# Scores and mix in smaller steps, the mask on the way out of PSUM, and norms by Ln, Exp and one Newton step, in a planned transformer kernel

## The chip, the cores and the metric

The kernel runs on one core of a Trainium2 chip. The time is the device time of one execution in microseconds (us); the time before is the median of three runs.

Five engines matter here. PE (TensorE) multiplies matrices and transposes; its products land in PSUM. DVE (VectorE), ACT (ScalarE) and POOL (GpSimd) work element by element, and SP issues transfers. Each engine runs its own list of instructions in order. An instruction whose input is not ready, or whose output buffer is still in use, holds up everything behind it in the same list.

## What is computed

Sixteen sequences of 256 tokens, 128 wide, go through two layers. The first part (a linear attention, a mixture of experts, and a causal linear attention with learned features) is not touched by the change. The last part is a stack of six blocks of windowed attention and a gated feed-forward layer, and the change is in its attention:

```python
def attn_layer(x, Wqkv, qs, ksc, Wo):
    q, k, v = ...                       # 16 heads of 64
    q = l2norm(q) * qs                  # l2norm(t) = t / max(norm(t), 1e-12)
    k = l2norm(k) * ksc
    q = q * cos * scale + rotate_half(q) * sin * scale
    k = k * cos / scale + rotate_half(k) * sin / scale
    out = local_attention(q, k, v)      # windows of 32, each sees itself and the one before
    return out @ Wo

# in local_attention
sim = einsum("bhwie,bhwje->bhwij", bq, bk2) * 8.0
sim = where(mask, -max_float, sim)
attn = softmax(sim, -1)
out = einsum("bhwij,bhwje->bhwie", attn, bv2)

for i in range(6):
    x = attn_layer(shift_tokens(x), ...) + x
    x = ffn_layer(shift_tokens(x), ...) + x
```

All arithmetic is in float32.

## The kernel before

Four stages follow each other. The first three (linear attention, experts, causal attention) take up to about 1650 us. The fourth is the stack of six blocks; there are 8 units of two sequences, and a sequence has two tiles of 128 tokens. So each block has 32 tiles in 8 units, and the whole stage has 192 tiles in 48 units.

The fourth stage is not written in the order in which it runs. Every piece of work is declared as a `Step` with its engine, a booked duration, the steps that it waits for, the buffers that it takes and a rank. `Plan.run` then plays a clock through these booked durations and lets each free engine take the ready step of lowest rank whose buffers are free. What comes out is a fixed list per engine, emitted in a manual schedule (L1155). A finished step makes its successors ready after `LAG` (L68), 0.12 us for every engine; a switch of ACT's function table is booked at `SWITCH`, 1.3 us. The plan's clock decides the lists only; on the chip the engines wait for each other by semaphores, by the real durations. Buffers come in kinds with few slots (L694 to L709): four PSUM pairs of 1024 columns, two `e`, four `t1`, two `sq` and so on. A step that takes a PSUM pair can start only when the steps that use its earlier content are through. Work on a later tile is let in three tiles ahead (`AHEAD`, and `gate` at L1114).

One tile goes through these steps, the names being those of the code:

- `projections` (L738): PE multiplies the 128 tokens by the weights of q, and then of k, into a PSUM pair each (L748). ACT squares the pair (L801), DVE multiplies it by the cosine table (`first`, L755) and, with halves swapped, by the sine table (`second`, L762), and reduces the squares per head (L771). POOL adds the two products (L810).
- `norms` (L773) calls `inv_norm` (L724) on DVE for q and k together, 128 by 32 values: a floor (L726), a first guess from the bits of the number (L729), and three Newton steps of three instructions (L733 to L735). POOL scales q and k by it (L777), PE transposes both (L783), ACT copies them to `qT` and `kT` (L789).
- `attention` (L836): `scores` (L843) is one PE step with 64 small products; 32 tokens see 64 keys, for 16 heads and 4 windows. DVE adds the mask in PSUM (`mask`, L860), takes the maximum per row (`top`, L864), and subtracts it on the way to `e` in SBUF (`below`, L869). ACT takes the exponential (L878).
- PE multiplies the value products (L885), ACT copies them to `va` (L892); PE transposes `e` (L899), ACT copies that to `eT` (L956). `mix` (L904) is 32 small products for each half of the heads (L911), two PE steps per tile. DVE divides by the sums (`divide`, L922 and L923), PE transposes, ACT copies to `oT` (L929).
- Per sequence `output` (L979) multiplies by Wo (L985) and DVE adds to the residual (L994). Per unit `feed_forward` (L1000) follows, with a norm, three gates with the gelu function on ACT, and products on PE (L1011, L1044, L1064).

In the records a float32 product shows as two MATMUL rows and two weight loads (LDWEIGHTS, engine PEld). ACT's table loads are put in when the program is built, ahead of a function that is not in the table loaded last.

Of the kernel before, what the change touches and what calls it, by code (L numbers as in the profile page):

```python
# [17 lines left out]
P = 128  # L18
# [31 lines left out]
class Step:  # L50


    def __init__(self, eng, work, fn, after, takes, uses, rank, table):
        self.eng, self.work, self.fn, self.rank = eng, work, fn, rank
        self.takes, self.uses, self.table = takes, uses, table
        self.next, self.wait = [], 0
        for b in (*takes, *uses):
            b.left += 1
        for s in after:
            s.next.append(self)  # L60
            self.wait += 1


class Plan:

    LAG = 0.12  # L68
    SWITCH = 1.3

    def __init__(self, slots):
        self.slots, self.steps, self.tick = slots, [], 0
        self.free = {k: list(range(len(v))) for k, v in slots.items()}

    def step(self, eng, work, fn, after=(), takes=(), uses=(), rank=0, table=None):
        s = Step(eng, work, fn, [a for a in after if a is not None], takes, uses, rank, table)
        self.steps.append(s)
        return s
# [30 lines left out]
    def run(self):  # L109
# [5 lines left out]
        for n, s in enumerate(self.steps):  # L115
# [3 lines left out]
            if not s.wait:  # L119
                heapq.heappush(ready[s.eng], (s.rank, n, s))  # L120
        now, table, opened = 0.0, None, {}
        left = len(self.steps)
        self.log = []
        while left:
            moved = True
            while moved:
                moved = False
                for eng, heap in ready.items():
# [40 lines left out]
                    at[eng] = now + work  # L169
                    heapq.heappush(events, (now + work + self.LAG, count, got))  # L170
                    heapq.heappush(events, (now + work, count + 1, None))
# [3 lines left out]
            while events and events[0][0] <= now:  # L175
# [31 lines left out]
def tile_kernel(ctx: ExitStack, tc: tile.TileContext, a: dict, out: bass.AP):  # L207
# [469 lines left out]
    with ExitStack() as st:  # L677
# [45 lines left out]

        def inv_norm(x, n):  # L724

            dve.tensor_scalar(x, x, 1e-24, None, ALU.max)  # L726
            y = sd.tile([P, n], F32, name="d_ny")
            t = sd.tile([P, n], F32, name="d_nt")
            dve.tensor_scalar(  # L729
                y.bitcast(I32), x.bitcast(I32), -0.5, 1597463007.0, ALU.mult, ALU.add  # L730
            )
            for _ in range(3):
                dve.tensor_tensor(t, y, y, ALU.mult)  # L733
                dve.scalar_tensor_tensor(t, t, -0.5, x, ALU.mult, ALU.mult)
                dve.scalar_tensor_tensor(y, t, 1.5, y, ALU.add, ALU.mult)  # L735
            return y

        def projections(q, t):  # L738
# [33 lines left out]

            def norms():  # L773
                o.rn = inv_norm(o.ss.rearrange("p g h -> p (g h)"), 2 * HEADS)

# [17 lines left out]
            for qk in range(2):  # L793
                pj, sq, t1, t2 = Buf("pair"), Buf("sq"), Buf("t1"), Buf("t2")
                mm = step(
                    "pe", 1.72, partial(product, qk, pj), [*q.ready, *q.loaded, q.gate(t)],
                    [pj], rank=rank,
                )
# [21 lines left out]
            for qk in range(2):  # L820
                dst, off = (q.kT, WIN + t * P) if qk else (qT, 0)
                pz = Buf("pair")
                m = step("pool", 1.9, partial(scale, qk, t1s[qk]), [nm, adds[qk]], [], [t1s[qk]], rank)
                tn = step("pe", 0.88, partial(turn, t1s[qk], pz), [m], [pz], [t1s[qk]], rank)
# [11 lines left out]
        def attention(q, t):  # L836
# [5 lines left out]

            def scores():  # L843

                for c in range(8):
                    for par in range(2):
# [11 lines left out]
            def mask():  # L858
                s3 = pS.t.rearrange("p (h k) -> p h k", k=2 * WIN)
                dve.tensor_tensor(s3, s3, bc(win[:, t, :], [P, HEADS, 2 * WIN], 1), ALU.add)  # L860

            def top():
                o.m = sd.tile([P, HEADS], F32, name="d_m")
                dve.tensor_reduce(  # L864
                    o.m, pS.t.rearrange("p (h k) -> p h k", k=2 * WIN), AX.X, ALU.max
                )

            def below():
                dve.tensor_tensor(  # L869
                    e.t.rearrange("p c a k -> p a c k"),  # L870
                    pS.t.rearrange("p (a c k) -> p a c k", a=2, k=2 * WIN),
                    bc(o.m.rearrange("p (a c) -> p a c", a=2), [P, 2, 8, 2 * WIN], 3),
                    ALU.subtract,
                )

# [27 lines left out]

            def mix(hh, po):  # L904
                for k in range(4):
                    c = 4 * hh + k
# [26 lines left out]

            sc = step("pe", 1.9, scores, [o.done[0], *q.turned[: t + 1]], [pS], [qT, kT], rank)
            mk = step("dve", 1.15, mask, [sc], [], [pS], rank)
            tp = step("dve", 1.15, top, [mk], [], [pS], rank)
            be = step("dve", 1.15, below, [tp], [e], [pS], rank)
            ex = step("act", 0.98, exps, [be], [], [e], rank, ("exp", 0))
            q.soft.append(be)
            vs = []  # L940
            for b2 in range(NB // 2):
                pv = Buf("pair")
                v = step(
                    "pe", 1.94, partial(values, b2, pv), [*q.ready, *q.loaded, mk], [pv], [], rank
                )
# [6 lines left out]
            pz = Buf("pair")  # L952
            te = step("pe", 0.88, partial(turn, e, pz), [ex], [pz], [e], rank)
            pe_ = step(
# [4 lines left out]
            for hh in range(2):  # L959
                po = Buf("pair")  # L960
                mx = step("pe", 0.75, partial(mix, hh, po), [pe_, *vs], [po], [eT, va], rank)
                ds.append(
                    step(
                        "dve", 0.85, partial(divide, hh, po), [mx],
                        [] if hh else [y], [po] + ([y] if hh else []), rank,
                    )
                )
            py = Buf("pair")
            ty = step("pe", 0.88, partial(turn, y, py), ds, [py], [y], rank)
            if t == 0:  # L970
# [8 lines left out]
        def output(q):  # L979
# [16 lines left out]
            rank = q.rank + 1  # L996
            mm = step("pe", 3.5, product, [*q.outs, *q.loaded], [pr], [q.oT], rank)
            return step("dve", 0.9, add, [mm], [], [pr], rank)
# [267 lines left out]
```

## Time and profile before

| | us |
|---|---|
| median of three runs (lowest, highest) | 5855.04 (5848.07, 5859.02) |
| the profiled execution, its own time | 5849.97 |
| its span in the profile | 5848.2 |
| PE busy | 4866.8 (83%) |
| DVE busy | 4182.3 (72%) |
| ACT busy | 2325.8 (40%) |
| POOL busy | 1951.1 (33%) |

Busy times are sums over the whole span. A matmul's end is modelled, so that a busy PE is not PE at its peak. The groups of instructions (line, engine, operation, output and input, count; busy us and mean ns of one; idle time before them and what ended it) give the durations of the fourth stage:

```profile
L810 POOL TENSOR_TENSOR d_t<-d_t,d_t 128x1024 f32<-128x1024 f32 x384 | 905.3, 2363 | 1717.1 <-DVE d_t L762 1242.4
L777 POOL TENSOR_TENSOR d_t<-d_t,d_ny 128x1024 f32<-128x1024 f32 x384 | 722.7, 1903 | 520.4 <-DVE d_ny L735 515.9
L771 DVE TENSOR_REDUCE d_ss<-d_sq 128x16 f32<-128x1024 f32 x384 | 464.9, 1211 | 1.4
L851 PE MATMUL pp<-d_kT,d_qT 64*32 64x64 f32 x24576 | 309.2, 232 | 157.2 <-issue 103.8
L911 PE MATMUL pp<-d_va,d_eT 64*32 64x65 f32 x24576 | 301.1, 228 | 85.5 <-issue 41.5
```

"issue" is time in which the engine waited for nothing that the profile shows.

### The profile page before, as it was taken

The page shows a single profiled execution, that of the slowest core. Times are in us where ns is not written, and L with a number is a line of the kernel's source. Part 1 is how long each engine was busy: PE and PEld are TensorE (multiplying, and loading weights), DVE is VectorE, ACT ScalarE, POOL GpSimd, SP SyncE. Part 2 cuts the span into 40 slices and gives each one's busy share as a digit, 9 for nine tenths or more (in the row PEclk, how much of TensorE's full clock was granted, in tenths as well). Part 3 has the DMA queues.
Part 4 walks back from the last instruction along what each step waited for, and adds up shares of the span by engine and source line. Part 5 has one row for each costly group of instructions (what it writes and reads, how often), then busy time and mean ns, then how long its engine had stood idle before and what let it go on. Part 6 is the DMA issues. An engine that isn't in the chain of part 4 may idle for free. (4 is left out here: it accounts for less than half of the span.)

```text
span 5848.2 us, 153345 instructions
## 1 busy us (share of the span) xinstructions
PE 4866.8 (83%) x69216; PEld 3086.3 (53%) x69216; DVE 4182.3 (72%) x7764; ACT 2325.8 (40%) x2701; POOL 1951.1 (33%) x964
## 2 busy tenths in 40 slices
PE   4677778787788888888888888898898888888886
PEld 3444566566655555555555555555555555555554
DVE  3333777777777777777678777777777777777775
ACT  1343112111134444444444444444444444444443
POOL 0000222222234344344344334334334434434432
PEclk7898899999999999999999999999999999999998
DMA  1000000000000000000000000000000000000001
GB/s 37 13 1 20 1 2 2 4 3 2 2 25 2 2 2 13 10 2 2 2 17 6 2 2 2 21 2 2 2 2 21 2 2 2 2 2 2 2 2 30
DMA packets 29195, 40.16 MB, mean 7 GB/s; under 512 B 5118, under 2 KB 24060, under 8 KB 27772
## 3 DMA queue, kind: packets, MB, share of 16 engines
q1 hardware_dynamic: 28540, 30.35, 1.7%
q8 instruction: 543, 8.90, 0.6%
q14 instruction: 112, 0.92, 0.1%
HBM read 26.15 MB, written 4.19 MB: 5 GB/s over the span
## 5 line engine op out<-in xcount | busy, mean ns | idle before, releaser
L810 POOL TENSOR_TENSOR d_t<-d_t,d_t 128x1024 f32<-128x1024 f32 x384 | 905.3, 2363 | 1717.1 <-DVE d_t L762 1242.4
L777 POOL TENSOR_TENSOR d_t<-d_t,d_ny 128x1024 f32<-128x1024 f32 x384 | 722.7, 1903 | 520.4 <-DVE d_ny L735 515.9
L748 PE MATMUL pp<-d_wqkv,xs 128*128 128x512 f32 x1536 | 776.4, 636 | 85.0 <-ACT d_oT L929 49.6
L885 PE MATMUL pp<-d_wqkv,xs 128*64 128x512 f32 x3072 | 753.5, 624 | 76.2 <-DVE d_t L762 75.2
L755 DVE TENSOR_TENSOR d_t<-pp,d_tab 128x1024 f32<-128x1024 f32 x384 | 467.8, 1218 | 392.7 <-PE pp L748 392.6
L801 ACT ACTIVATE d_sq<-pp 128x1024 f32<-128x1024 f32 x384 | 388.6, 1025 | 756.2 <-PE pp L748 250.6
L892 ACT COPY d_va<-pp 128x1024 f32<-128x1024 f32 x384 | 383.5, 1011 | 530.5 <-PE pp L885 529.5
L783 PE MATMUL pp<-ident,d_t 128*128 128x128 f32 x3072 | 414.0, 282 | 119.5 <-ACT d_qT L789 85.3
L762 DVE TENSOR_TENSOR d_t<-pp,d_tab 128x1024 f32<-128x1024 f32 x384 | 467.1, 1216 | 50.3 <-ACT d_sq L801 50.3
L783 PEld LDWEIGHTS pp<-ident,d_t 128*128 128x128 f32 x3072 | 354.3, 145 | 246.3 <-issue 158.9
L569 POOL TENSOR_TENSOR c_e<-c_e,c_sm 128x2048 f32<-128x2048 f32 x64 | 231.7, 3621 | 757.0 <-DVE c_sm L568 682.1
L748 PEld LDWEIGHTS pp<-d_wqkv,xs 128*128 128x128 f32 x1536 | 279.4, 200 | 375.5 <-issue 228.9
L771 DVE TENSOR_REDUCE d_ss<-d_sq 128x16 f32<-128x1024 f32 x384 | 464.9, 1211 | 1.4
L885 PEld LDWEIGHTS pp<-d_wqkv,xs 128*64 128x64 f32 x3072 | 202.2, 142 | 489.1 <-issue 344.1
L851 PE MATMUL pp<-d_kT,d_qT 64*32 64x64 f32 x24576 | 309.2, 232 | 157.2 <-issue 103.8
L851 PEld LDWEIGHTS pp<-d_kT,d_qT 64*32 64x32 f32 x24576 | 266.1, 108 | 225.0 <-issue 158.9
L911 PE MATMUL pp<-d_va,d_eT 64*32 64x65 f32 x24576 | 301.1, 228 | 85.5 <-issue 41.5
L985 PE MATMUL pp<-d_oT,d_wo 128*128 128x256 f32 x1536 | 357.1, 385 | 1.8 <-ACT d_oT L929 1.3
L911 PEld LDWEIGHTS pp<-d_va,d_eT 64*32 64x32 f32 x24576 | 261.1, 106 | 180.6 <-issue 90.7
L564 ACT ACTIVATE c_e<-c_e 128x2048 f32<-128x2048 f32 x64 | 122.4, 1912 | 566.2 <-DVE c_e L562 552.3
L985 PEld LDWEIGHTS pp<-d_oT,d_wo 128*128 128x128 f32 x1536 | 284.0, 190 | 113.0 <-ACT f_h L1051 38.5
L929 ACT COPY d_oT<-pp 128x1024 f32<-128x1024 f32 x192 | 193.9, 1010 | 331.7 <-PE pp L899 252.3
(172 smaller groups left out, 8440.2 us busy)
## 6 DMA issues: line engine op xcount, KB each, us to landing
d_wqkv<-L_ffn_Wqkv SPq DMA_DIRECT2D x6, 1536.0 KB, 7.1
d_wo<-L_ffn_Wo SPq DMA_DIRECT2D x6, 512.0 KB, 4.0
xin<-L_attn_x SPq DMA_DIRECT2D x8, 256.0 KB, 2.9
keep<-xu SPq DMA_DIRECT2D x8, 256.0 KB, 2.0
d_y<-keep SPq DMA_DIRECT2D x8, 256.0 KB, 2.7
out<-d_y SPq DMA_DIRECT2D x8, 256.0 KB, 2.3
d_w<-L_ffn_W SPq DMA_DIRECT2D x6, 341.0 KB, 3.0
b_w<-b_w SPq DMA_DIRECT2D x3, 576.0 KB, 7.4
```

Of the source, the lines that this page charges most:

```text
L748: pe.matmul(pj.t[:, hf * 512 : (hf + 1) * 512], lhsT=xj, rhs=q.w["qkv"][:, c : c + 512], start=True, stop=True,)
L755: dve.tensor_tensor(t1.t, heads(pj.t), bc(q.lay.tab[:, 0, t, cc], hs, 1), ALU.mult)
L762: dve.tensor_tensor(t2.t.rearrange("p h (x d) -> p h x d", x=2), swapped(pj.t), bc(q.lay.tab[:, 1, t, cc].rearrange("p (x d) -> p x d", x= ...
L771: dve.tensor_reduce(o.ss[:, qk, :], sq.t, AX.X, ALU.add)
L777: pool.tensor_tensor(t1.t, t1.t, bc(o.rn[:, qk * HEADS : (qk + 1) * HEADS], hs, 2), ALU.mult)
L783: pe.transpose(pz.t[:, c * P : (c + 1) * P], t1.t[:, 2 * c : 2 * c + 2, :].rearrange("p h d -> p (h d)"), ident,)
L801: lambda sq=sq, pj=pj: act.activation(sq.t, heads(pj.t), AF.Square),
L810: lambda t1=t1, t2=t2: pool.tensor_tensor(t1.t, t1.t, t2.t, ALU.add),
L851: pe.matmul(pS.t[b * WIN : (b + 1) * WIN, s0 : s0 + 2 * WIN], lhsT=qT.t[r, c, b * WIN : (b + 1) * WIN], rhs=kT.t[r, c, k0 : k0 + 2 * WIN], ...
L885: pe.matmul(pv.t[par * DH : (par + 1) * DH, j * 512 : (j + 1) * 512], lhsT=q.x[:, x0 : x0 + 2 * WIN], rhs=wv[:, par, :, :], start=True, st ...
L911: pe.matmul(po.t[b * WIN : (b + 1) * WIN, s0 : s0 + DH + 1], lhsT=eT.t[r, c, b * WIN : (b + 1) * WIN], rhs=va.t[r, b, c, :], start=True, s ...
L985: pe.matmul(pr.t[:, :SEQ], lhsT=q.w["o"][:, c, :], rhs=q.oT.t[:, c, :], start=(c == 0), stop=(c == 7),)
```

## The change

The plan gets a lag for each engine in place of one for all, and a limit for PE: steps carry a count of instructions, and a step of more than 32 is held back while more than `BLOCK` instructions would fall into the last `SPAN` microseconds of the plan's clock. The scores become four PE steps of 16 products, the mix four steps of 16 (two per half). The mask is added on the way from PSUM to `e`, the maximum is taken from `e`, and the subtraction of the maximum is done in place on `e` by POOL. The norms become a floor on DVE, Ln and Exp with scale -0.5 on ACT, and one Newton step on DVE. The value products wait for the scores and no longer for the mask. The stages before and after the planned one are the same. Some booked durations are set anew. All lists of the fourth stage are laid out anew by the plan.

```diff
-    LAG = 0.12
+    LAG = {"pe": 0.25, "act": 0.15, "dve": 0.12, "pool": 0.15, "sp": 2.0}
     SWITCH = 1.3
+    BLOCK, SPAN = 256, 3.6
...
+                        if s.count > 32 and self._dense(s, now, past, events):
+                            back.append(item)
+                            continue
...
+    def _dense(self, s, now, past, events):
+        room = self.BLOCK - s.count
+        for t, c in reversed(past):
+            room -= c
+            if room < 0:
+                wait = t + self.SPAN - s.work
+                if wait > now + 1e-6:
+                    self.unique -= 1
+                    heapq.heappush(events, (wait, self.unique, None))
+                    return True
+                return False
+        return False
...
-            def norms():
-                o.rn = inv_norm(o.ss.rearrange("p g h -> p (g h)"), 2 * HEADS)
+            def floor():
+                o.ss = o.ss.rearrange("p g h -> p (g h)")
+                dve.tensor_scalar(o.ss, o.ss, 1e-24, None, ALU.max)
+
+            def guess():
+                o.rn = sd.tile([P, 2 * HEADS], F32, name="d_rn")
+                act.activation(o.rn, o.ss, AF.Ln)
+                act.activation(o.rn, o.rn, AF.Exp, scale=-0.5)
+
+            def refine():
+                r = sd.tile([P, 2 * HEADS], F32, name="d_rt")
+                dve.tensor_tensor(r, o.rn, o.rn, ALU.mult)
+                dve.scalar_tensor_tensor(r, r, -0.5, o.ss, ALU.mult, ALU.mult)
+                dve.scalar_tensor_tensor(o.rn, r, 1.5, o.rn, ALU.add, ALU.mult)
...
-            nm = step("dve", 2.5, norms, reds, rank=rank)
+            fl = step("dve", 0.22, floor, reds, rank=rank)
+            gu = step("act", 0.45, guess, [fl], rank=rank, table=("exp", 0))
+            nm = step("dve", 0.68, refine, [gu], rank=rank)
...
-            def scores():
-                for c in range(8):
+            def scores(g):
+                for c in (2 * g, 2 * g + 1):
...
             def mask():
-                s3 = pS.t.rearrange("p (h k) -> p h k", k=2 * WIN)
-                dve.tensor_tensor(s3, s3, bc(win[:, t, :], [P, HEADS, 2 * WIN], 1), ALU.add)
+                dve.tensor_tensor(
+                    e.t.rearrange("p c a k -> p a c k"),
+                    pS.t.rearrange("p (a c k) -> p a c k", a=2, k=2 * WIN),
+                    win[:, t, :].unsqueeze(1).unsqueeze(1).to_broadcast([P, 2, 8, 2 * WIN]),
+                    ALU.add,
+                )
...
             def below():
-                dve.tensor_tensor(
-                    e.t.rearrange("p c a k -> p a c k"),
-                    pS.t.rearrange("p (a c k) -> p a c k", a=2, k=2 * WIN),
-                    bc(o.m.rearrange("p (a c) -> p a c", a=2), [P, 2, 8, 2 * WIN], 3),
-                    ALU.subtract,
-                )
+                e3 = e.t.rearrange("p c a k -> p (c a) k")
+                pool.tensor_tensor(e3, e3, bc(o.m, [P, HEADS, 2 * WIN], 2), ALU.subtract)
...
-            def mix(hh, po):
-                for k in range(4):
+            def mix(hh, g, po):
+                for k in (2 * g, 2 * g + 1):
...
-            sc = step("pe", 1.9, scores, [o.done[0], *q.turned[: t + 1]], [pS], [qT, kT], rank)
-            mk = step("dve", 1.15, mask, [sc], [], [pS], rank)
-            tp = step("dve", 1.15, top, [mk], [], [pS], rank)
-            be = step("dve", 1.15, below, [tp], [e], [pS], rank)
+            sc = []
+            for g in range(4):
+                sc.append(
+                    step(
+                        "pe", 0.48, partial(scores, g), [o.done[0], *q.turned[: t + 1], *sc[-1:]],
+                        [] if g else [pS], [qT, kT] + ([pS] if g else []), rank, count=64,
+                    )
+                )
+            mk = step("dve", 1.15, mask, sc, [e], [pS], rank)
+            tp = step("dve", 1.14, top, [mk], [], [e], rank)
+            be = step("pool", 1.95, below, [tp], [], [e], rank)
```

The floor is L788 in the new listing, Ln and Exp L792 and L793, the refinement L797 to L799, the scores L878, the mask L886, the maximum L895, the subtraction L901, the exponential L905, the value copy L919, the mix L938.

More of the change, by code (lines that the diff above doesn't have):

```diff
@@ L50, with __init__ @@
 class Step:
-    def __init__(self, eng, work, fn, after, takes, uses, rank, table):
+    def __init__(self, eng, work, fn, after, takes, uses, rank, table, count):
         self.eng, self.work, self.fn, self.rank = eng, work, fn, rank
+        self.count = count
         self.takes, self.uses, self.table = takes, uses, table
@@ L73, in __init__, with step @@
         self.free = {k: list(range(len(v))) for k, v in slots.items()}
-    def step(self, eng, work, fn, after=(), takes=(), uses=(), rank=0, table=None):
-        s = Step(eng, work, fn, [a for a in after if a is not None], takes, uses, rank, table)
+    def step(self, eng, work, fn, after=(), takes=(), uses=(), rank=0, table=None, count=0):
+        after = [a for a in after if a is not None]
+        s = Step(eng, work, fn, after, takes, uses, rank, table, count)
         self.steps.append(s)
@@ L121, in run @@
         now, table, opened = 0.0, None, {}
+        past = []
         left = len(self.steps)
         self.log = []
+        self.unique = 0
         while left:
@@ L169, in run @@
                     at[eng] = now + work
-                    heapq.heappush(events, (now + work + self.LAG, count, got))
+                    if got.count:
+                        past.append((now, got.count))
+                        del past[:-40]
+                    heapq.heappush(events, (now + work + self.LAG[eng], count, got))
                     heapq.heappush(events, (now + work, count + 1, None))
@@ L722, in swapped @@
             return ap.rearrange("p (h x d) -> p h x d", x=2, d=DH // 2)[:, :, ::-1, :]
[L724 to L730, printed above, removed]
-            )
[L732 to L736, printed above, removed]
         def projections(q, t):
@@ L795, in projections @@
                 mm = step(
-                    "pe", 1.72, partial(product, qk, pj), [*q.ready, *q.loaded, q.gate(t)],
-                    [pj], rank=rank,
+                    "pe", 1.76, partial(product, qk, pj), [*q.ready, *q.loaded, q.gate(t)],
+                    [pj], rank=rank, count=8,
                 )
@@ L823, in projections @@
                 m = step("pool", 1.9, partial(scale, qk, t1s[qk]), [nm, adds[qk]], [], [t1s[qk]], rank)
-                tn = step("pe", 0.88, partial(turn, t1s[qk], pz), [m], [pz], [t1s[qk]], rank)
+                tn = step("pe", 0.88, partial(turn, t1s[qk], pz), [m], [pz], [t1s[qk]], rank, count=16)
                 new = [dst] if (qk == 0 or t == 0) else []
@@ L864, in top @@
                 dve.tensor_reduce(
-                    o.m, pS.t.rearrange("p (h k) -> p h k", k=2 * WIN), AX.X, ALU.max
+                    o.m, e.t.rearrange("p c a k -> p (c a) k"), AX.X, ALU.max
                 )
             def below():
-                dve.tensor_tensor(
-                    e.t.rearrange("p c a k -> p a c k"),
-                    pS.t.rearrange("p (a c k) -> p a c k", a=2, k=2 * WIN),
-                    bc(o.m.rearrange("p (a c) -> p a c", a=2), [P, 2, 8, 2 * WIN], 3),
-                    ALU.subtract,
-                )
+                e3 = e.t.rearrange("p c a k -> p (c a) k")
+                pool.tensor_tensor(e3, e3, bc(o.m, [P, HEADS, 2 * WIN], 2), ALU.subtract)
             def exps():
@@ L943, in attention @@
                 v = step(
-                    "pe", 1.94, partial(values, b2, pv), [*q.ready, *q.loaded, mk], [pv], [], rank
+                    "pe", 1.94, partial(values, b2, pv), [*q.ready, *q.loaded, sc[-1]], [pv], [], rank, count=16,
                 )
@@ L952, in attention @@
             pz = Buf("pair")
-            te = step("pe", 0.88, partial(turn, e, pz), [ex], [pz], [e], rank)
+            te = step("pe", 0.88, partial(turn, e, pz), [ex], [pz], [e], rank, count=16)
             pe_ = step(
@@ L960, in attention @@
                 po = Buf("pair")
-                mx = step("pe", 0.75, partial(mix, hh, po), [pe_, *vs], [po], [eT, va], rank)
+                mx = []
+                for g in range(2):
+                    mx.append(
+                        step(
+                            "pe", 0.38, partial(mix, hh, g, po), [pe_, *vs, *mx], [] if g else [po],
+                            [eT, va] + ([po] if g else []), rank, count=64,
+                        )
+                    )
                 ds.append(
                     step(
-                        "dve", 0.85, partial(divide, hh, po), [mx],
+                        "dve", 0.85, partial(divide, hh, po), mx,
                         [] if hh else [y], [po] + ([y] if hh else []), rank,
@@ L968, in attention @@
             py = Buf("pair")
-            ty = step("pe", 0.88, partial(turn, y, py), ds, [py], [y], rank)
+            ty = step("pe", 0.88, partial(turn, y, py), ds, [py], [y], rank, count=16)
             if t == 0:
@@ L996, in output @@
             rank = q.rank + 1
-            mm = step("pe", 3.5, product, [*q.outs, *q.loaded], [pr], [q.oT], rank)
+            mm = step("pe", 3.5, product, [*q.outs, *q.loaded], [pr], [q.oT], rank, count=32)
             return step("dve", 0.9, add, [mm], [], [pr], rank)
```

## The prediction

> **What bounds the kernel.** I read the busy shares first, then the 40 slices, then a table of windows over the planned stage, then the waits of PE there, and last the line of time around single waits. The page says
>
> ```profile
> PE 4866.8 (83%) x69216; PEld 3086.3 (53%) x69216; DVE 4182.3 (72%) x7764; ACT 2325.8 (40%) x2701; POOL 1951.1 (33%) x964
> ```
>
> but the change touches only the planned stage, about 1655 to 5800 us. The transposes of L1011, one group per unit of four tiles, start first at 1751.7 and last at 5795.9, so a unit takes (5795.9 - 1751.7) / 47 = 86.05 us and a tile 21.5. In that stage:
>
> ```profile
> 1700.00:5750.00 4050.00, 3538.23 (x61521) 2144.16 (x61520) 3053.80 (x5553) 1887.80 (x1978) 1635.98 (x799) 0.97 0.02 5
> ```
>
> PE is busy 87%, DVE 75%, ACT 47%, POOL 40%: per tile 18.8, 16.2, 10.0 and 8.7 us. PE's list is in a fixed order, so the stage is PE's work plus whatever that list waits for. The longest of PE's waits between 1700 and 5800 us (total, times, longest):
>
> ```profile
> PE pp L851 <- issue: 103.8, 61, 2.6
> PE pp L783 <- ACT d_qT L789: 84.2, 45, 2.1
> PE pp L885 <- DVE d_t L762: 75.2, 59, 2.4
> PE pp L851 <- ACT d_kT L789: 50.7, 46, 1.1
> PE pp L748 <- ACT d_oT L929: 49.6, 45, 1.1
> PE pp L911 <- ACT d_eT L956: 41.5, 39, 1.3
> PE pp L911 <- issue: 40.5, 36, 2.5
> ```
>
> All rows of that answer add to 527 us, 11.1 per unit (4100 / 86.05 = 47.6 units). "Issue" rows, in which PE waited for no other engine, are 150 us, 3.15 per unit; waits for ACT, DVE and POOL are 377 us, 7.9 per unit. Where an issue wait falls is seen here (start, duration, idle before):
>
> ```profile
> 2094.33 1.47 PE L911 MATMUL pp<-d_va,d_eT 64*32 64x65 f32 x127
> ...
> 2095.62 1.38 PE L851 MATMUL pp<-d_kT,d_qT 64*32 64x64 f32 x118
> 2098.76 0.31 PE L851 MATMUL pp<-d_kT,d_qT 64*32 64x64 f32 x7 [1.76 <-issue]
> ```
>
> 128 records of the mix (64 products, two records each) and 121 of the scores run in 2.7 us, each record with a weight load of its own, and then PE stands for 1.76 us in the middle of a group. Lone groups of 128 records (1.48 us) mostly pass: PE stopped on issue at the scores 61 times in 192 tiles.
>
> A wait costs more than its length. Four windows around a 2.0 us wait (length; busy of PE, PEld, DVE, ACT, POOL; clock):
>
> ```profile
> 2150.00:2152.40 2.40, 2.36 (x59) 0.81 (x40) 2.09 (x11) 0.00 (x0) 0.14 (x1) 1.00 0.02 7
> 2152.40:2154.40 2.00, 0.00 (x0) 0.00 (x0) 2.00 (x3) 1.01 (x1) 2.00 (x2) 1.00 0.00 0
> 2154.40:2157.90 3.50, 3.46 (x8) 0.69 (x8) 3.50 (x4) 0.00 (x0) 3.50 (x2) 0.53 0.00 0
> 2157.90:2160.00 2.10, 2.10 (x19) 2.01 (x18) 2.10 (x3) 1.95 (x3) 0.44 (x1) 0.98 0.00 0
> ```
>
> After the idle 2.0 us, 3.4 us run at half clock. The same follows the issue wait above (clock 0.50 from 2100.0 to 2103.4). In half-microsecond windows from 2000 to 2350 us I find 8 such stretches, two per unit; one of 3.4 us loses 1.7. The Trainium skill, "TensorE: Matmul & The Clock Gate", section "Why this matters for your kernels", warns only of idle gaps over about 3 us; by that rule no wait here (longest 2.6, but for one of 7.3) would cost clock. By the rows 1.5 to 2 us suffice, so shorter stalls count for about double. I take the rows.
>
> **DVE loses work.** Per tile: L729 (0.18) goes, nine Newton instructions become three (192 ns and 35 ns between them: 6 x 0.227 = 1.36), and the subtraction L869 (1.22) goes. Mask and maximum keep their size: the mask writes SBUF as L869 did (1218 ns against 1228), the maximum reads SBUF as L771 does (1211 against 1220). Sum -2.8 us: 16.2 to 13.5 per tile. DVE does not bound, so this is worth something only in the waits of PE for DVE (75 us at L885, 22 at L748, 20 at L783, 10 for d_y): at most 2.7 us per unit with POOL's and ACT's rows aside.
>
> **POOL gains the subtraction.** Not in the trace; the nearest row is L777, 128x1024 with one broadcast input, 1903 ns; L810 with two full inputs (2363) is the other bound, and below 1903 nothing speaks. I take 1.9: POOL 8.7 to 10.6 per tile, half idle. But it is in order behind the adds (2.36) and scalings (1.9 each), so the exponentials get their input 1 to 3 us later than from DVE; behind them stand the transposes of e and the mix. With three tiles in flight I count part of this below.
>
> **Norms: ACT gains.** Ln and Exp over 128x32 are not in the trace. Lower bound a DVE instruction of that size, 0.19; the nearest ACT row (128x128 L473, 369 ns) is the upper; I take 0.22 each. The greater cost is in the built program: ACT's list has 458 table loads where it had 113. Every tile has one before Ln and one before Exp (192 each), while loads before the softmax exponential fall from 47 to 8. Here a rule speaks for the change: the Trainium skill, "ScalarE: Activation LUTs", section "Table sets: the hidden batching unit", says that ln followed by exp takes one load, since one set holds both. The built order names two different sets, so the rule does not hold here; had it, 192 loads and 246 us would be gone. For the price of a load the same page, section "What ACT_TABLE_LOAD costs", gives 1283 ns plus a drain, 2.66 us in all; the trace has
>
> ```profile
> 4025.96 1.28 ACT L878 ACT_TABLE_LOAD   x1 [9.14 <-DVE d_e L869]
> 4027.26 1.06 ACT L878 ACTIVATE d_e<-d_e 128x1024 f32<-128x1024 f32 x1
> ```
>
> 1.28 us and then 0.02 us to the next instruction. By the row 345 loads more are 443 us of ACT, 2.3 per tile; by the page 918 us, 4.8 per tile. I take the row: ACT 10.0 + 2.3 + 0.4 = 12.8 us per tile, still not the bound. The plan, however, books 0.45 us for Ln and Exp together, so everything that ACT does behind them comes up to 2.6 us later than the order was made for.
>
> How much of it PE sees depends on its place. Two places from the new order. First: ACT's list has put kT, load, Ln, load, Exp, exponential of e; PE's has, after that kT, 32 score products (0.7), one projection pair (1.8), then the transposes of e. ACT needs 1.28 + 0.22 + 1.28 + 0.22 + 1.06 = 4.1, PE has 2.5 of work: PE stands 1.6 us. Second: the load before Ln stands behind an ACT that is idle for 3 us, and DVE has the two adds of an output product, 3.6 us of PE later, between the floor and the first refining instruction: no wait at all. DVE also stops at that instruction until Exp is through; in 53 of 192 tiles nothing lies between floor and refining (stop of 2 to 3 us), in 60 one instruction (1 to 2 us), in 79 more. Masks and rotations of other tiles are queued behind it, and PE wants their PSUM pairs.
>
> I added such places up along two stretches of the new order, about a unit each, with the durations of the rows and 0.1 to 0.4 us per hand-over: 7.4 us of PE waiting to 74.8 of work, and 11.9 to 77.4. A unit has 71.2 us of work at full clock, so 0.127 x 71.2 = 9.0 us, against 7.9 now. That is an estimate by hand. Without the second set it would be some 4 lower.
>
> **Products in steps.** The same 128 small products per tile (64 scores, 64 mix), but as eight groups of 16 (with weight loads 64 instructions) between long products, and by the plan not over 256 instructions in 3.6 us. Starting a small group behind a long product shows no cost (L1044 to L851 at 2035.17: 1.81 us after the start of two 512-wide products, as between long ones). I count nine tenths of the issue waits as gone, 2.8 per unit. If PE after a wait runs several groups together, they come back, up to 3.15. The plan's new lags lay every list out afresh; nothing in the trace prices that alone, and I take it with the walk above.
>
> **The sum**, per unit: issue waits -2.8; other waits 9.0 - 7.9 = +1.1; half clock: one of the two stretches followed an issue wait (-1.7), the new waits of 1.5 us and more bring half of that back, -0.85. Together -2.55 x 48 = -122 us. The profiled execution took 5849.97 us, span 5848.2; 5849.97 - 122 = 5728. The median of the runs is 5 us above it, so 5733; I say 5730.
>
> **Rivals.**
> 1. As summed, 5620 to 5810: 0.50.
> 2. The loads mostly fall into ACT's idle half (53% of the stage) and DVE's relief shows: other waits 5.5 instead of 9.0, both clock stretches shorter (-0.85 more): 5730 - 4.35 x 48 = 5520. For it: a load without input can run before Ln's data is there. Against: ACT's lists in the two stretches were busy up to the load about half the time. 0.20.
> 3. Slower: the loads set the pace. In its own list ACT delivers q, k, e and values late, DVE stops at the refinement, and PE waits on both. If 0.7 of 2 x 1.283 x 192 = 493 us gets to PE, that is +345, and one low-clock stretch more per unit (+80): 5855 - 135 + 425 = 6145; at half, with the clock as now, 5855 - 135 + 246 = 5966, which I take as its time. Against the gain on issue it decides from 135 / 493 = 27% on. For it: 113 tiles with little or nothing between floor and refinement, and a plan that knows of none of this. Against: the walk above already has the delays in it. 0.25.
> 4. The limit is not what stops PE, and cut groups stop as before: -0.4 instead of -2.8 and no gain of clock: 5730 + 3.2 x 48 = 5885; with an in-between outcome, no change: 0.05.
>
> About 0.2% (12 us) is what a measurement of this kernel can tell from no change. Faster 0.70, within 0.04, slower 0.26. The range takes in most of rival 2 and the lower half of rival 3: 5550 to 5930.
>
> **What would show it.** L878 and L938 after "issue" under 30 us together; 384 loads of 1.28 us at L792 and L793, or 2.66 if the page is right; PE waiting for d_e, d_eT and d_kT of ACT more than now; DVE waiting at L797 for ACT by 150 to 300 us; POOL's L901 at 1.9; clock in the stage 0.96 to 0.98. I am wrong if DVE and PE waits behind Ln exceed 5 us per unit more than now, or if the issue waits stay.

## The result, and the profile after

The change made the kernel slower by 0.2%: 5866.38 us, median of 20 runs, against 5854.07 of 20 runs of before; the ratio is 1.0022, with a 95% interval of 1.0015 to 1.0029. The prediction was 5730.

First the busy shares of the page of after, then its window of the planned stage (length; busy of PE, PEld, DVE, ACT, POOL with counts; clock, DMA share, GB/s):

```profile
PE 4933.5 (84%) x69216; PEld 3077.6 (52%) x69216; DVE 3804.5 (65%) x6228; ACT 2863.6 (49%) x3430; POOL 2315.3 (39%) x1156
```

```profile
1700.00:5750.00 4050.00, 3583.86 (x61214) 2118.23 (x61212) 2677.82 (x4027) 2401.53 (x2674) 1988.90 (x984) 0.97 0.02 5
```

Per tile of 21.55 us, ACT and POOL moved as reckoned, to 12.8 and 10.6 us. DVE fell from 16.2 to 14.2 and not to 13.5; the last section has a part of the reason. PE is busy 46 us more in the same 4050 us, though it did slightly less of the same work (61214 records instead of 61521). The first transposes of the residual (L1052) start at 1771.5 and the last at 5823.1: 86.2 us per unit against 86.05. Once it runs, the stage is as fast as it was; it starts up about 20 us later. In a_no_tables below, with the same lists and no loads for the norms, the first transposes start at 1758.7, so that most of the delay seems to go with the table loads. The longest waits of PE between 1700 and 5800 us in after (total, times, longest):

```profile
PE pp L938 <- ACT d_eT L990: 90.1, 71, 3.0
PE pp L926 <- ACT d_e L905: 56.7, 54, 1.9
PE pp L808 <- DVE d_z L949: 44.0, 23, 1.9
PE pp L808 <- POOL d_t L802: 35.4, 37, 2.1
PE pp L760 <- ACT d_va L919: 27.3, 15, 1.8
...
PE pp L938 <- issue: 12.1, 6, 2.2
...
PE pp L878 <- issue: 9.0, 7, 2.1
```

The issue waits fell from 150 to 21 us, and in their place PE waits for the softmax path (L905, L990). On the other engines stand the table loads (groups of ACT) and what DVE waits for behind them (waits of DVE):

```profile
L792 ACT ACT_TABLE_LOAD x189 | 242.5, 1283 | 3.4
L793 ACT ACT_TABLE_LOAD x189 | 242.5, 1283 | 3.3
L792 ACT ACTIVATE d_rn<-d_ss 128x32 f32<-128x32 f32 x189 | 43.4, 229 | 127.9 <-DVE d_ss L788 126.3
```

```profile
DVE d_rt L797 <- ACT d_rn L793: 307.6, 151, 4.9
```

To compare orders I split each run's time per tile into three. Tiles are PE's records from 1700 to 5400 us over 326.5 a tile; the clock is the mean of half-microsecond windows from 2000 to 3500 us. *Work* is PE's busy time times that clock, *clock* the rest of its busy time, *waits* its idle time. "Cut" means scores and mix in small steps. i_pow_whole, which POOL bounds, is left out. us per tile:

| run | period | work | clock | issue waits | other waits |
|---|---|---|---|---|---|
| before | 21.47 | 18.09 | 0.66 | 0.81 | 1.91 |
| after (cut) | 21.59 | 18.50 | 0.59 | 0.10 | 2.40 |
| a_no_tables (cut) | 20.80 | 18.41 | 0.41 | 0.08 | 1.90 |
| b_norms_dve (cut) | 20.91 | 18.58 | 0.24 | 0.02 | 2.07 |
| c_whole | 20.17 | 18.08 | 0.19 | 0.50 | 1.40 |
| d_below_dve (cut) | 22.58 | 18.37 | 1.32 | 0.11 | 2.78 |
| e_booked (cut) | 22.22 | 18.43 | 0.63 | 0 | 3.16 |
| g_before_lag | 21.88 | 17.95 | 1.26 | 0.56 | 2.11 |
| h_dve_whole | 21.02 | 18.09 | 0.44 | 0.49 | 2.00 |
| j_no_limit (cut) | 21.98 | 18.30 | 0.85 | 0.24 | 2.59 |
| l_scores_whole | 21.77 | 18.04 | 0.81 | 0.41 | 2.51 |
| m_mix_whole (scores cut) | 22.50 | 18.42 | 0.93 | 0.28 | 2.88 |
| o_before_split (cut) | 21.10 | 18.41 | 0.30 | 0.06 | 2.34 |
| p_after_26 (cut) | 21.45 | 18.30 | 0.71 | 0.16 | 2.28 |
| p_whole_26 | 20.22 | 18.04 | 0.29 | 0.50 | 1.39 |
| q_whole_no_tables | 19.73 | 18.07 | 0.19 | 0.52 | 0.95 |
| r_late_whole | 21.97 | 17.95 | 0.90 | 0.28 | 2.84 |
| s_after_lag20 (cut) | 21.71 | 18.56 | 0.30 | 0.17 | 2.68 |
| s_whole_lag20 | 22.21 | 18.04 | 0.86 | 0.51 | 2.79 |

Two things limit the table. The stretch takes in the later start: 20 us over its 171 tiles make up the 0.12 by which the period of after is longer. And work and clock depend on where the clock is read. From the transposes of the fifth unit to those of the forty-fifth (160 tiles), with the clock of just that stretch, the period goes from 21.62 to 21.65: work 18.18 to 18.48, clock 0.68 to 0.66, issue waits 0.80 to 0.11, other waits 1.96 to 2.40. Differences of 0.1 between rows mean little.

### The profile page after: what moved, and what is told of

Read it like the earlier page. It is cut to its first block, busy times and chain, and to the rows that moved or that the text cites. A ratio compares the mean times of both kernels' runs of the same rounds, so it can differ in the third digit from the quotient of the medians.

```text
span 5875.5 us, 152494 instructions
## 1 busy us (share of the span) xinstructions
PE 4933.5 (84%) x69216; PEld 3077.6 (52%) x69216; DVE 3804.5 (65%) x6228; ACT 2863.6 (49%) x3430; POOL 2315.3 (39%) x1156
## 5 line engine op out<-in xcount | busy, mean ns | idle before, releaser
L802 POOL TENSOR_TENSOR d_t<-d_t,d_rn 128x1024 f32<-128x1024 f32 x384 | 723.3, 1903 | 462.3 <-DVE d_rn L799 459.7
L760 PE MATMUL pp<-d_wqkv,xs 128*128 128x512 f32 x1536 | 764.8, 623 | 62.4 <-ACT d_va L919 27.3
L912 PE MATMUL pp<-d_wqkv,xs 128*64 128x512 f32 x3072 | 742.6, 615 | 31.4 <-DVE d_t L774 20.0
L919 ACT COPY d_va<-pp 128x1024 f32<-128x1024 f32 x384 | 385.9, 1010 | 349.3 <-PE pp L912 337.1
L808 PE MATMUL pp<-ident,d_t 128*128 128x128 f32 x3072 | 454.6, 299 | 120.2 <-DVE d_z L949 44.0
L901 POOL TENSOR_TENSOR d_e<-d_e,d_m 128x1024 f32<-128x1024 f32 x192 | 366.0, 1906 | 316.0 <-DVE d_m L895 234.9
L808 PEld LDWEIGHTS pp<-ident,d_t 128*128 128x128 f32 x3072 | 374.3, 153 | 197.2 <-issue 90.2
L938 PE MATMUL pp<-d_va,d_eT 64*32 64x65 f32 x24576 | 336.8, 228 | 128.2 <-ACT d_eT L990 91.2
L760 PEld LDWEIGHTS pp<-d_wqkv,xs 128*128 128x128 f32 x1536 | 267.8, 193 | 309.4 <-issue 204.2
L938 PEld LDWEIGHTS pp<-d_va,d_eT 64*32 64x32 f32 x24576 | 260.9, 107 | 316.8 <-ACT d_eT L990 164.5
L912 PEld LDWEIGHTS pp<-d_wqkv,xs 128*64 128x64 f32 x3072 | 198.7, 139 | 400.2 <-issue 290.1
L878 PE MATMUL pp<-d_kT,d_qT 64*32 64x64 f32 x24576 | 372.6, 230 | 34.6 <-ACT d_kT L814 25.7
L878 PEld LDWEIGHTS pp<-d_kT,d_qT 64*32 64x32 f32 x24576 | 269.9, 109 | 224.5 <-issue 165.8
L1026 PE MATMUL pp<-d_oT,d_wo 128*128 128x256 f32 x1536 | 354.1, 384 | 8.3 <-ACT d_oT L956 8.3
L1026 PEld LDWEIGHTS pp<-d_oT,d_wo 128*128 128x128 f32 x1536 | 290.0, 191 | 95.1 <-ACT d_oT L956 35.3
```

The lines of the kernel that those rows point to most:

```text
L760: pe.matmul(pj.t[:, hf * 512 : (hf + 1) * 512], lhsT=xj, rhs=q.w["qkv"][:, c : c + 512], start=True, stop=True,)
L802: pool.tensor_tensor(t1.t, t1.t, bc(o.rn[:, qk * HEADS : (qk + 1) * HEADS], hs, 2), ALU.mult)
L808: pe.transpose(pz.t[:, c * P : (c + 1) * P], t1.t[:, 2 * c : 2 * c + 2, :].rearrange("p h d -> p (h d)"), ident,)
L878: pe.matmul(pS.t[b * WIN : (b + 1) * WIN, s0 : s0 + 2 * WIN], lhsT=qT.t[r, c, b * WIN : (b + 1) * WIN], rhs=kT.t[r, c, k0 : k0 + 2 * WIN], ...
L912: pe.matmul(pv.t[par * DH : (par + 1) * DH, j * 512 : (j + 1) * 512], lhsT=q.x[:, x0 : x0 + 2 * WIN], rhs=wv[:, par, :, :], start=True, st ...
L938: pe.matmul(po.t[b * WIN : (b + 1) * WIN, s0 : s0 + DH + 1], lhsT=eT.t[r, c, b * WIN : (b + 1) * WIN], rhs=va.t[r, b, c, :], start=True, s ...
```

## The experiments

Every ratio is against runs of the kernel before on the same chip (5834 to 5850 us there), with its 95% interval; after itself is at 1.0022. Unless it is said otherwise, the plan lays out all lists anew.

**a_no_tables.** Ln and Exp without their tables, all orders kept.

```diff
-                act.activation(o.rn, o.ss, AF.Ln)
-                act.activation(o.rn, o.rn, AF.Exp, scale=-0.5)
+                act.activation(o.rn, o.ss, AF.Identity, scale=0.01)
+                act.activation(o.rn, o.rn, AF.Identity, scale=0.5)
```

> The changed kernel, with Ln and Exp of the norms replaced by two Identity activations of the same 128x32 tiles (scales 0.01 and 0.5); the norms are left out by this, their instructions are not. PE, DVE and POOL have the same lists as the changed kernel, ACT the same list without 345 table loads. Theory L (the table loads make ACT late, DVE stands at the refinement and PE waits behind both): DVE's wait at L797 falls from 308 us to under 60, PE's waits for ACT and DVE from 450 us between 1700 and 5750 us to about 300, time 5866 - 150 = 5715 (5650 to 5780). Theory H (what was gained on issue waits is spent on the starts of the small product groups; the loads are hidden): 5850 to 5866.

Measured 5721.03 us, ratio 0.9804 (0.9790 to 0.9817). DVE's wait behind Exp, in the waits of DVE of this run:

```profile
DVE d_rt L797 <- ACT d_rn L793: 50.0, 69, 1.5
```

Theory L holds for the loads: the same lists without 345 loads are some 130 us faster (2.2% of 5837.72), and PE's other waits are back at 1.90 per tile.

**b_norms_dve.** The norms of before on DVE, the rest of the change kept.

```diff
-            fl = step("dve", 0.22, floor, reds, rank=rank)
-            gu = step("act", 0.45, guess, [fl], rank=rank, table=("exp", 0))
-            nm = step("dve", 0.68, refine, [gu], rank=rank)
+            nm = step("dve", 2.5, norms, reds, rank=rank)
```

> The changed kernel with the norms of before, eleven instructions on DVE, no Ln and Exp; planned anew. DVE works 1.5 us more per tile, ACT 3.0 less. Theory L: like the run without loads, less some waits for a busier DVE: 5740 (5680 to 5800). Theory H: no gain from ACT, DVE busier: 5860 to 5900.

Measured 5737.82, ratio 0.9836 (0.9822 to 0.9849), as theory L had it. With the cut, moving the norms off DVE lost about 110 us, the new order included: no sign that DVE was what PE was short of.

**c_whole.** Scores in one step, mix in two, so no limit.

```diff
-            def scores(g):
-                for c in (2 * g, 2 * g + 1):
+            def scores():
+                for c in range(8):
...
-            def mix(hh, g, po):
-                for k in (2 * g, 2 * g + 1):
+            def mix(hh, po):
+                for k in range(4):
```

> The changed kernel with the scores in one PE step and the mix in two, as before, and so without the limit; planned anew. Theory H: issue waits of PE come back from 21 us to 120 to 160, and the starts of five groups per tile fall away, 5 x 0.1 x 192 = 96 us: 5866 + 120 - 96, so 5860 to 5910. If the small groups start for nothing, as the prediction had it: 5866 + 130 + 40 for the clock = 6030 (5990 to 6070).

Measured 5594.35, ratio 0.9587 (0.9573 to 0.9601), outside all that was expected: 4.1% faster than before and 250 us faster than after. Neither theory, starts for nothing or starts that eat the gain, can give that. PE's waits from 1700 to 5400 us:

```profile
PE pp L926 <- ACT d_e L905: 141.3, 160, 1.9
PE pp L878 <- issue: 74.2, 42, 2.4
PE pp L808 <- ACT d_va L919: 28.3, 42, 0.7
PE pp L808 <- POOL d_t L802: 16.0, 46, 0.8
```

Issue waits came back, as they should (0.10 to 0.50 per tile), but PE's waits for DVE nearly vanished (0.91 to 0.18), and with them most of the half-clock stretches (0.59 to 0.19).

**d_below_dve.** The subtraction of the maximum on DVE, and booked there.

```diff
-                pool.tensor_tensor(e3, e3, bc(o.m, [P, HEADS, 2 * WIN], 2), ALU.subtract)
+                dve.tensor_tensor(e3, e3, bc(o.m, [P, HEADS, 2 * WIN], 2), ALU.subtract)
...
-            be = step("pool", 1.95, below, [tp], [], [e], rank)
+            be = step("dve", 1.15, below, [tp], [], [e], rank)
```

> The changed kernel with the subtraction of the maximum on DVE (in place on e in SBUF) and not on POOL; planned anew. DVE works 1.2 us more per tile, POOL 1.9 less. Theory P (the exponentials come late because POOL's list holds the subtraction up): PE's waits for d_e and d_eT, 147 us now, fall by half, time 5790 (5750 to 5830). Theory L: no gain, DVE stands before the refinement with one instruction more behind it: 5860 to 5930.

Measured 6054.43, ratio 1.0377 (1.0363 to 1.0391). Theory P is not borne out: here POOL's subtraction goes with some 200 us of gain, not of loss. What part of that is the order can't be told from this run.

From here theory S was on trial: a score pair in PSUM stays open while other work of PE stands between its steps (in the trace of after, 5.5 us of it in the median), and four pairs are few.

**j_no_limit.** `BLOCK` from 256 to 1 << 20.

> The changed kernel with the steps as they are, but with no limit on instructions (256 made a million); planned anew. Theory S (a score pair stays open while other work of PE stands between its four steps, 5.4 us of it on average in the changed order, so that one of four PSUM pairs is held, and PE waits for DVE and for a free pair; the limit is what pushes the steps apart): time falls most of the way to the run with whole steps, 5650 (5600 to 5720), with issue waits of 60 to 130 us. If the steps drift apart without the limit too: 5830 to 5880.

Measured 5942.56, ratio 1.0186 (1.0172 to 1.0200). Slower than after, with 0.24 us of issue waits per tile instead of 0.10. Nothing here says that the limit harms, though the order is another one too.

**e_booked.** `gu = step("act", 3.1, ...)` in place of 0.45.

> The changed kernel with Ln and Exp of the norms booked at 3.1 us in the plan, as they take with their two loads, in place of 0.45; planned anew, instructions the same. Theory L in its form 'the plan does not know of the loads': DVE's wait at L797 falls from 308 us to under 100, time 5866 - 80 = 5780 (5740 to 5820). Theory S: little, 5830 to 5870, since the open pairs stay.

Measured 5994.20, ratio 1.0277 (1.0258 to 1.0296). DVE's wait at L797 fell to 47 us, as expected, and the time rose by some 150: PE now waits for DVE (1.36 us per tile) and ACT (1.46). Telling the plan the true price took one wait away and led to a slower order.

**g_before_lag.** The kernel before with the new `LAG`.

> The kernel before with the new lags alone; planned anew, instructions the same. If the lags carry a part of the gain of the run with whole steps (better timed lists): 5790 (5740 to 5830). If the lists of before were as good: 5840 to 5870.

Measured 5889.27, ratio 1.0099 (1.0084 to 1.0114), above both expectations. In this order the lags alone are no gain: PE waits 0.73 us per tile for POOL's scaled tiles, where before had a single such wait, of 7.3 us.

**i_pow_whole.** As c_whole, the norms by POOL's power.

```diff
-            gu = step("act", 0.45, guess, [fl], rank=rank, table=("exp", 0))
-            nm = step("dve", 0.68, refine, [gu], rank=rank)
+            nm = step("pool", 1.3, power, [fl], rank=rank)
```

> The changed kernel with whole steps for scores and mix, and the norms as one power of -0.5 on POOL after the floor, booked 1.3 us; no Ln, Exp, refinement or loads of tables. Theory L and S together: 5594 less what the loads still cost there (DVE's wait at L797 is 170 us between 1700 and 5400, PE's for d_e of ACT 141): 5500 (5440 to 5560), if the power over 128x32 costs POOL no more than 2 us. If it costs by element, 1 us per 4 columns as in the row of 128x4, 8 us per tile, POOL bounds and the time is over 5700.

Measured 6397.00, ratio 1.0967 (1.0952 to 1.0982), the case of a price by element. The groups of POOL show why:

```profile
L261 POOL TENSOR_TENSOR d_rn<-d_ss,nhalf 128x32 f32<-128x32 f32 x192 | 1042.3, 5429 | 11.4 <-DVE d_ss L788 0.5
L261 POOL TENSOR_TENSOR f_rs<-f_ve,nhalf 128x4 f32<-128x4 f32 x48 | 48.4, 1009 | 17.6 <-DVE f_ve L1043 17.6
```

**l_scores_whole and m_mix_whole.** Only the scores whole, only the mix whole (the edits of c_whole one at a time).

> The changed kernel with the scores in one PE step, the mix still in four; planned anew. Theory S (PE's other work between the steps of the scores, 5.4 us on average, keeps a PSUM pair open, and each start of a small group costs 0.1 to 0.19 us): the scores are the larger part, since no work stands inside their group now and starts per tile fall from 4.2 to 2.3; 5594 + a quarter to a third of the way, 5660 (5600 to 5720). Theory C (the order that the plan finds falls out better or worse by 2% whatever is changed): anywhere from 5600 to 6000.

> The changed kernel with the mix in two PE steps as before, the scores still in four; planned anew. Theory S: 4.7 us of other work still stand inside the group of scores, starts fall only from 4.2 to 3.7: 5800 (5750 to 5860). Theory C: anywhere from 5600 to 6000.

Measured 5893.36, ratio 1.0088 (1.0072 to 1.0104), and 6044.13, ratio 1.0347 (1.0329 to 1.0366). Each half of c_whole is slower than after, and together they are 250 us faster. No sum of fixed costs of the edits does that.

**o_before_split.** The kernel before with the cut and the limit alone.

> The kernel before with only the cut of scores and mix and the limit, old lags, norms, mask and subtraction as before; planned anew. Theory S: issue waits fall by about 130 us, starts rise from 1.5 to 3.3 per tile and a score pair is open for 3.8 us longer: slower than before by 50 to 200 us, 5900 to 6050. The prediction's view (starts cost nothing, issue waits and their clock are gained): 5855 - 135 - 40 = 5680.

Measured 5785.21, ratio 0.9906 (0.9890 to 0.9922). Theory S fell here: the cut alone made before faster by 0.9%. Issue waits went from 0.81 to 0.06 per tile, work rose from 18.09 to 18.41. The prediction's 5680 was too good by about that work, and by other waits that rose from 1.91 to 2.34.

**h_dve_whole.** As c_whole, with the norms of before on DVE.

> The changed kernel with whole steps for scores and mix and the norms of before on DVE: of the change there remain the mask on the way to SBUF, the subtraction on POOL, and the lags; planned anew. Theory L: without the loads faster than the whole steps with Ln and Exp: 5594 - 60 = 5534 (5480 to 5580). If the loads are hidden once PSUM pairs are not short: 5594 to 5640, since DVE has 1.5 us more per tile.

Measured 5765.66, ratio 0.9862 (0.9842 to 0.9882). Slower than c_whole by some 160 us, though it loads no tables; with the cut the same exchange was 110 us faster. Again the sign depends on the rest.

The next runs tell the edits from the order in which the plan puts them.

**r_late_whole.** The orders of after kept; the last step of a group emits all of it.

```diff
-                for c in (2 * g, 2 * g + 1):
+                for c in range(8) if g == 3 else ():
...
-                for k in (2 * g, 2 * g + 1):
+                for k in range(4) if g == 1 else ():
```

> The changed kernel with its own plan and orders, but the first three steps of the scores emit nothing and the fourth all 64 products, and the first step of a mix nothing and the second all 32. DVE, ACT and POOL have the same lists, PE the same but for the place of the products. This prices the cut alone. From the accounts of the runs so far, per tile: work of PE at full clock 18.5 to 18.1 (-0.4), issue waits 0.1 to 0.5 (+0.4), and masks about 1 us later behind a burst of 1.4 us. If the cut is worth little in itself: 5840 to 5900. If it is the cause of the 250 us (theory S): under 5750.

Measured 5942.37, ratio 1.0176 (1.0159 to 1.0193). In the orders of after, whole groups in the last place are worse by about 90 us. PE goes from long to small products 2.2 times per tile instead of 4.2, and work fell by 0.55 us per tile: in kept orders, that is what the cut costs. But issue waits rose by 0.18, other waits by 0.44 and the clock's loss by 0.31. So c_whole did not win by being whole alone.

**q_whole_no_tables.** The two Identity activations of a_no_tables, in c_whole, orders kept.

> The run with whole steps for scores and mix (5594), with Ln and Exp replaced by Identity (scales 0.01 and 0.5), so that the norms are left out and no table is loaded for them; all lists the same but for the loads. It prices the loads in the fastest order. If they cost what they cost in the changed order (130 us): 5465 (5430 to 5500). If an order with slack hides them: 5550 to 5590.

Measured 5504.34, ratio 0.9426 (0.9410 to 0.9441): 1.6% below c_whole, about 95 us, between the two expectations. The loads cost 0.44 us per tile in this order and 0.79 in that of after, nearly all of it in waits and clock.

**p_after_26 and p_whole_26.** PE's lag 0.26 instead of 0.25, in after and in c_whole.

> The changed kernel with the plan's lag of PE at 0.26 in place of 0.25: no instruction changes, every list is ordered anew. Theory C (which order the plan falls into is worth some per cent): more than 40 us off 5851, the changed kernel on this chip, on either side. If the edits decide: within 20 us of it.

> The run with whole steps for scores and mix (5594) with the plan's lag of PE at 0.26 in place of 0.25: no instruction changes, the lists are ordered anew. Theory C: more than 40 us off 5594, and more likely slower (5640 to 5850), since 5594 is the best of 12. If the edits decide: within 20 us of 5594.

Measured 5839.18, ratio 0.9998 (0.9989 to 1.0007), and 5607.23, ratio 0.9601 (0.9588 to 0.9614). Both stay within 13 us of their twins, so theory C's 40 us did not come: a push of 0.01 us in the plan moves little, though it changes the lists (466 table loads in place of 458).

**s_after_lag20 and s_whole_lag20.** Lag 0.20 for PE, ACT, DVE and POOL.

> The run with whole steps for scores and mix (5594) with the plan's lag at 0.20 for PE, ACT, DVE and POOL alike; no instruction changes, the lists are ordered anew. If whole steps lead the plan to orders in which PE seldom waits for DVE, whatever the lags: 5580 to 5660, waits for DVE under 0.4 us per tile. If 5594 is one family of orders that the lags 0.25 and 0.26 share (theory C): over 5700.

> The changed kernel, cut and all, with the plan's lag at 0.20 for PE, ACT, DVE and POOL alike; no instruction changes, the lists are ordered anew. If the cut keeps the plan from good orders: 5800 to 5950. If the order is chance (theory C): it may as well be under 5750.

Measured 5967.94, ratio 1.0199 (1.0183 to 1.0215), for the whole steps, and 5894.17, ratio 1.0076 (1.0062 to 1.0091), with the cut. The same declared steps that took 5594 us take some 360 us more in another order. (ACT's loads follow from its order: 481 here, 452 in c_whole. All other instructions are the same.) So whole steps do not make every order a good one, as theory C had it; with the cut, 5894 lies where it was expected if the cut keeps the plan from good orders, which one run can't show. PE's waits in s_whole_lag20 from 1700 to 5400 us, to be held against those of c_whole:

```profile
PE pp L878 <- ACT d_kT L814: 119.6, 42, 5.0
PE pp L808 <- POOL d_t L802: 57.3, 32, 3.5
PE pp L938 <- ACT d_eT L983: 55.2, 54, 2.0
PE pp L1012 <- ACT d_oT L956: 49.0, 44, 1.8
PE pp L878 <- issue: 42.2, 33, 2.5
```

Work (18.04 and 18.08) and issue waits (0.51 and 0.50) are equal; other waits are 2.79 against 1.40, and the clock's loss 0.86 against 0.19. The order, with the loads that it brings, moves 2 us of 20 per tile.

## Why the prediction was wrong

**The issue waits: right.** 2.8 us per unit were to go; 0.81 - 0.10 per tile, 2.84 per unit, went.

**Starting a small group "shows no cost": wrong, and the step that failed.** The prediction took 1.81 us, the start of two 512-wide products to that of a group, to be the time between long ones too. The trace of before has 1.72 there, in each of 42 such places:

```profile
2071.11 1.06 PE L783 MATMUL pp<-ident,d_t 128*128 128x128 f32 x8 [0.52 <-DVE d_e L869]
2072.01 1.88 PE L748 MATMUL pp<-d_wqkv,xs 128*128 128x512 f32 x4
2073.73 1.04 PE L899 MATMUL pp<-ident,d_e 128*128 128x128 f32 x8
```

So 0.1 us of cost stood in the quoted time. In after, the same pair of products (L760) shows a price on both sides, here with a group behind it, then with groups ahead and behind:

```profile
4207.23 0.66 PE L1052 MATMUL pp<-ident,xs 128*128 128x128 f32 x4
4207.72 1.88 PE L760 MATMUL pp<-d_wqkv,xs 128*128 128x512 f32 x4
4209.53 0.46 PE L938 MATMUL pp<-d_va,d_eT 64*32 64x65 f32 x32
```

```profile
4065.48 0.46 PE L878 MATMUL pp<-d_kT,d_qT 64*32 64x64 f32 x32
4065.87 1.98 PE L760 MATMUL pp<-d_wqkv,xs 128*128 128x512 f32 x4
4067.78 0.45 PE L878 MATMUL pp<-d_kT,d_qT 64*32 64x64 f32 x32
```

From start to start the pair takes 1.72 us in the median between transposes, 1.81 between transposes and a group (10 cases), 1.82 between a group and the output product L1026 (32 cases), and 1.91 between two groups (62 cases). The size of the group plays no part: behind transposes it is 1.81 ahead of 128 records (c_whole, 124 cases) as ahead of 32. A group of 32 itself takes 0.39 us, a quarter of 128 records 0.353. I estimate from this that each separate stretch of small products costs about 0.2 us, 0.1 going in and 0.1 coming out. (Between a group and L912, whose products are shown as 128*64, the pair takes 1.91 too, in 20 cases: small groups may not be the only ones with this price. That was not tested.) The new order has 4.2 stretches per tile, the old one 1.5; the 2.7 more are some 0.5 us by this estimate. As work the table has 18.30 to 18.58 where the scores are cut and 17.95 to 18.09 where they are whole, in every order tried; after less before is 0.41 us per tile there and 0.30 in the 160 tiles, so 1.2 to 1.6 us per unit, some 60 to 80 us over 192 tiles. The sum had it at zero.

**Other waits: right in kind, too small.** I walked to +1.1 us per unit; they rose by 0.44 to 0.49 per tile, 1.8 to 2.0 per unit. The loads are behind it as the walk said: a_no_tables brings the other waits back to 1.90. DVE's relief does not show in them. Against the "some 4 lower" per unit without the second set, the period fell by 0.79 per tile, 3.2 per unit, with both loads gone. The price of a load, 1283 ns with 3 us of idle time ahead of 189 loads in all, was that of the row and not the 2.66 us that the Trainium skill, "ScalarE: Activation LUTs", section "What ACT_TABLE_LOAD costs", gives with its drain. Its rule in "Table sets: the hidden batching unit", one load for ln and exp, did not come true in this build: both groups hold a load per tile. Rival 3 put the break-even at 27% of 493 us of loads reaching PE; by a_no_tables 130 us do, 26%.

**Clock: wrong.** 0.85 us per unit were to be won; at most 0.07 per tile, 0.3 per unit, was. Waits of 1.5 us and more fell from 127 to 91 between 1700 and 5400 us. But in before only 41 of the 127 were followed within 2 us by low clock (a half-microsecond window under 0.9), in after 38 of the 91. So a wait of that length can bring a half-clock stretch, as the prediction read it, and mostly doesn't; the fewer waits of after lose as much. What decides it stays open.

Together, per unit, in the 160 tiles: -2.8 (issue) + 1.8 (other waits) - 0.1 (clock) + 1.2 (starts) = +0.1, against the -2.55 of the sum; the later start of 20 us comes on top. (The table gives -2.84 + 2.0 - 0.3 + 1.6 = +0.5, with that start in it.) The span of the profiled runs grew by 27 us, the medians by 12: the profiled run of after was the slowest of its 20. So the gain on issue was real, and was given back to the starts of small groups and to waits behind table loads.

**What no step of mine allowed for** is the order. I took the plan's lists as if each edit had a price in them. The same steps took 5594 or 5968 us, or 5839 to 5994 with the cut, by what the plan was told. The experiments that keep the orders (a, q, r) give prices; those that edit and plan anew give a price and an order together. Of rival 4, in-between, the outcome was right and the reason was not: the cut did stop the issue waits.

What stays open: why the orders of c_whole and p_whole_26 are good ones. Their traces show the few waits for DVE (0.18 per tile in both); which place in the lists saves them was not found.

The best version tried is c_whole: the change without its cut, 0.9587 of before.

## What to carry to other kernels

Where a planner lays out the lists, price an edit in a kept order (swap or empty an instruction in place), and treat a time after planning anew as one draw: here the order was worth up to 6%. Before cutting a step into pieces, measure from start to start what a long product takes between long ones, ahead of a short piece and behind one, and multiply by the number of separate pieces; here it took back 60 to 80 of the 136 us that the cut won on issue. An activation of 0.23 us can bring a table load of 1.28 us: count the loads in the built list.

## What was not expected of the hardware

A group of small products costs 0.1 us on each side (1.72, 1.81 and 1.91 us above), whatever its size. Half-clock stretches came after some single waits of 1.5 us and more and not after others: 18 of 91 in c_whole (clock's loss 0.19 us per tile), 76 of 121 in s_whole_lag20 (0.86).

Some small instructions of DVE last until POOL's running instruction ends. In after:

```profile
1988.19 2.24 DVE L799 SCALAR_TENSOR_TENSOR d_rn<-d_rt,d_rn 128x32 f32<-128x32 f32 x1
1987.97 2.41 POOL L835 TENSOR_TENSOR d_t<-d_t,d_t 128x1024 f32<-128x1024 f32 x1 [0.34 <-DVE d_rt L797]
```

Without POOL at work L799 takes 0.19 us and the floor L788 0.17. Of 192 floors 102 take over 0.3 us (up to 2.1), and each of these ends within 0.1 us of the end of one of POOL's instructions; of the refinements, 13 at L797 and 22 at L799. L798 was not held in the 42 tiles in which POOL ran beside it (0.19). The cause was not tested. Before had 100 such floors, and none at L733 or L735, which ran beside POOL three times in all. Longer floors and refinements took about 0.4 us per tile of what DVE was to lose.

POOL's power took 5.43 us for 128x32 and 1.01 us for 128x4, about 0.16 us per column, where POOL's add takes 2.4 us for 1024 columns.
